# Cross-attention maxima added as three bfloat16 parts instead of two float32r parts

## The chip, the cores and the metric

The kernel is one launch on one core of a Trainium2 chip. The metric is the device time of that core in microseconds, as the median over several runs. Five engines share the work: TensorE (PE, with its weight loads shown apart as PEld), VectorE (DVE), ScalarE (ACT), GpSimd (POOL) and SyncE (SP), which here issues the DMAs. Each engine runs its own list of instructions, and the lists are tied together by semaphores.

## The reference

The kernel computes one decoder layer on 128 sequences of 128 tokens with 256 features. All three parts are added to the residual `x`:

```
x = x + self_attention(layernorm(x))               # 16 heads of 16, no mask
x = x + cross_attention(layernorm(x), ctx, ctx, mask)
x = x + ffn(layernorm(x))                          # 256 -> 1024 -> 256, ternary weights, GELU, layernorm inside

# cross-attention
scores = einsum('bhqd,bhkd->bhqk', Q, K) / sqrt(d_k)
scores = where(mask == 0, 1e-9, scores)            # mask: one row of keys, the same for all
attn   = softmax(scores)                           # exp(scores - max over keys) / sum
out    = einsum('bhqk,bhkd->bhqd', attn, V)
```

The softmax needs the maximum over the keys of every query and head. It is this maximum, negated, that the change handles.

## The kernel before

The sequences are taken in 32 groups of four (G = 4). Each group goes through self-attention, cross-attention and the FFN, and the three stages of different groups run side by side. All instructions are written out in a fixed order (`tc.manual_schedule()`): the string `ORDER` has one letter for each small step, `A` for a step of attention, `n`, `k`, `c` and `f` for the steps that prepare self-attention, prepare the keys of cross-attention, prepare its queries, and do the FFN of an earlier group. One pass over `ORDER` is one period: four rows of self-attention and four of cross-attention, a row being one sequence with all 16 heads. On each engine the instructions stand in the order in which this string emits them.

For a row, attention works in these steps, each emitted in one go:

- `maxima`: TensorE forms the scores with queries on the partitions (L562; in cross-attention after a mask term in bfloat16, L551), DVE takes the maximum over the keys, negated (L573), and writes it to `negm` (L579 for cross, L584 for self).
- `transposed_scores`: TensorE forms the scores again with the keys on the partitions (L620); in cross-attention DVE writes the constant into the masked places (`copy_predicated`, L630).
- `transposed_maxima`, for the row after: TensorE transposes `negm` into `pn`, a quarter of the one PSUM bank of `ps_av` (L589). For self-attention DVE adds it into the queries (`q_max`, L594). For cross-attention ACT copies it, rounded to float32r, to `first` (L604), and DVE forms `negm_t`: `pn` itself in the partitions of the first part, and `pn - first` in those of the second part (L606).
- `weights`: in cross-attention TensorE adds the maxima to the scores in PSUM with 16 small matmuls against the constant `add_max` (L644), four heads in each of four strips of 32 partitions. Then ACT takes the exponentials (L653, two halves).
- `outputs`: TensorE multiplies with the values into `av`, the same `ps_av` bank (L665), and ACT copies it out (L668).

`negm` has eight places of four heads in each strip; in cross-attention two of them hold the same maxima twice, so that the transposed tile holds the value twice, in different partitions. `add_max` picks and sums these partitions for each head.

The pools that matter are small. `ps_s` has room for the two score tiles of one row alone, so scores of the next row wait until the exponentials (or the maxima) have read the last ones. `ps_mm` has three banks, which all products of the projections and the FFN take in turn: `pq`, `pk`, `pv`, `po`, `pt`, `ph` (GELU on ACT, L392), `pg` (transposes L414, emptied by ACT L422 and DVE L424) and `py`. `ps_av` has one bank. The residual add of the output projection is DVE at L360, the statistics for the norms are DVE at L217 and L218, the copy of the values is L314 and that of the keys ACT at L300.

Of the kernel before, what the change touches and what calls it, by code (L numbers as in the profile page):

```python
# [18 lines left out]
F32 = mybir.dt.float32  # L19
F32R = mybir.dt.float32r  # L20
BF16 = mybir.dt.bfloat16
I32 = mybir.dt.int32
AF = mybir.ActivationFunctionType
ALU = mybir.AluOpType
AX = mybir.AxisListType
PSUM = bass.MemoryType.PSUM

P = 128
# [9 lines left out]
S4 = 4  # L38
# [21 lines left out]
def tile_decoder_layer(ctx: ExitStack, tc: tile.TileContext, a: dict, out: bass.AP):  # L60
    nc = tc.nc
    n_groups = a["x"].shape[0] // G

    const = ctx.enter_context(tc.tile_pool(name="const", bufs=1))
# [3 lines left out]
    p_att = ctx.enter_context(tc.tile_pool(name="p_att", bufs=2))  # L68
# [4 lines left out]
    ps_av = ctx.enter_context(tc.tile_pool(name="ps_av", bufs=1, space=PSUM))  # L73
# [32 lines left out]
    ident_strips = ident.rearrange("p (s r) -> p s r", s=S4)  # L106
# [4 lines left out]

    add_max = const.tile([P, 4, P], F32R, name="add_max")
    row_of = const.tile([P, 3], F32, name="row_of")
    for n in range(4):
        for i in range(2):
            rows = ident_strips[:, :, 4 * i + n]
            nc.vector.tensor_reduce(row_of[:, i : i + 1], rows, AX.X, ALU.add)
        nc.vector.tensor_tensor(row_of[:, 2:3], row_of[:, 0:1], row_of[:, 1:2], ALU.add)  # L120
        nc.vector.tensor_copy(add_max[:, n], row_of[:, 2:3].to_broadcast([P, P]))


    max_row = const.tile([P, CC, 2], F32, name="max_row")
# [1 line left out]
    for e in range(2):  # L126
        half = ident_strips[:, :, (1 - e) * HD : (1 - e) * HD + CC]
        nc.vector.tensor_reduce(max_rows[:, e : e + 1], half, AX.XY, ALU.add)
        for o in range(CC):
            nc.vector.tensor_reduce(max_row[:, o, e : e + 1], half[:, :, o], AX.X, ALU.add)  # L130
    minus_second = const.tile([P, 1], F32, name="minus_second")
    nc.vector.tensor_reduce(minus_second, ident_strips[:, :, 4:8], AX.XY, ALU.add, negate=True)

# [59 lines left out]
    rows = p_one.tile([P, S4, P], I32, name="rows", tag="g_0")  # L195
# [5 lines left out]
    least = const.tile([P, 1], F32, name="least")  # L201
# [337 lines left out]
    def score_tiles(name):  # L539
        return [ps_s.tile([P, 2, 4, P], F32, name=name, tag="s") for _ in range(2)]  # L540

    def maxima(stage, b, j):

        qt, kt = ready[stage, b]["q"], ready[stage, b]["k"]
        tok = slice(j * P, (j + 1) * P)
        s = score_tiles("s")
        if stage == "cross":
            for c in range(S4):
                for r in range(S4):
                    strip = slice(r * 32, (r + 1) * 32)  # L550
                    nc.tensor.matmul(  # L551
                        s[r // 2][c * 32 : (c + 1) * 32, r % 2],
                        ident_b[strip],
                        never[strip, c, None, :].to_broadcast([32, 4, P]),
                        start=True,
                        stop=False,
                        skip_group_check=True,
                    )
        for o in range(CC):
            for r in range(S4):  # L560
                strip = slice(r * 32, (r + 1) * 32)
                nc.tensor.matmul(  # L562
                    s[r // 2][:, r % 2, 2 * o : 2 * o + 2],
                    qt[strip, o, tok],
                    kt[strip, o, :, tok],
                    start=(stage == "self"),
                    stop=True,
                    skip_group_check=True,
                )

        mx = p_stat.tile([P, S4, 4, 2], F32, name="mx", tag="mx")[:, :, :, 0]
        for half in range(2):
            nc.vector.tensor_reduce(  # L573
                mx[:, 2 * half : 2 * half + 2], s[half], AX.X, ALU.max, negate=True
            )
        negm = negms[stage]
        if stage == "cross":
            twice = mx[:, :, None, :].to_broadcast([P, S4, 2, 4])
            nc.vector.tensor_scalar(negm[:, :, 0:2], twice, least, None, ALU.min)  # L579
        else:  # L580
            halves = negm.rearrange("p s a b -> p s (a b)").rearrange("p s (h d) -> p s h d", d=HD)
            heads = mx.rearrange("p s (o e) -> p s o e", e=2)
            for e in range(2):
                nc.vector.tensor_copy(halves[:, :, 1 - e, 0:CC], heads[:, :, :, e])  # L584
        return negm

    def transposed_maxima(stage, b, j, negm):
        pn = ps_av.tile([P, 4, P], F32, name="pn", tag="av")[:, 3]
        nc.tensor.transpose(pn, negm.rearrange("p s k n -> p (s k n)"), ident)  # L589
        if stage == "self":  # L590
            qt = ready[stage, b]["q"][:, :, j * P : (j + 1) * P]
            q_max = p_att.tile([P, CC, 2, P], F32, name="q_max", tag="q_max", bufs=1)
            for e in range(2):
                nc.vector.scalar_tensor_tensor(  # L594
                    q_max[:, :, e],
                    pn[:, None, :].to_broadcast([P, CC, P]),
                    max_rows[:, e : e + 1],
                    qt,
                    ALU.mult,
                    ALU.add,  # L600
                )
            return q_max
        first = p_att.tile([P, P], F32R, name="first", tag="q_max", bufs=1)
        nc.scalar.copy(first, pn)  # L604
        negm_t = p_att.tile([P, P], F32R, name="negm_t", tag="negm_t")
        nc.vector.scalar_tensor_tensor(  # L606
            negm_t, first.bitcast(F32), minus_second, pn, ALU.mult, ALU.add
        )
        return negm_t

    def transposed_scores(stage, b, j, added):
# [68 lines left out]
    def attention():  # L680
        w_t = added = None
        for i in range(-1, 2 * G * (n_groups + 1) + 1):
            here, following, before = row(i), row(i + 1), row(i - 1)
            cross = i % (2 * G) >= G
            if following:
                negm = maxima(*following)
            if i >= 0:
                yield
            if before:
                outputs(*before, w_t)  # L690
            if i >= 0:
                yield
            if here:
                s = transposed_scores(*here, added)
                if not cross:
                    w_t = weights(here[0], s, None)
            if i >= 0:
                yield
            added_here = added
            if following:  # L700
                added = transposed_maxima(*following, negm)
            if i >= 0:
                yield
            if cross and i >= 0:
                if here:
                    w_t = weights(here[0], s, added_here)
                yield
# [76 lines left out]
```

## Time and profile before

| | us |
|---|---|
| time, median of 3 runs | 2844.08 |
| lowest and highest of them | 2841.91, 2845.41 |
| the profiled execution: time | 2845.54 |
| the profiled execution: span | 2843.5 |
| mean granted TensorE clock in it | 0.98 of full |
| PE busy | 2723.7 (96%) |
| DVE busy | 2045.6 (72%) |
| ACT busy | 1546.9 (54%) |
| POOL busy | 1371.8 (48%) |

The profile comes from one execution of the program. A group is all instructions of one line, engine and operation; its row gives the busy time of all, the mean of one in ns, and the idle time of the engine just before them with what ended it. A timeline row gives the start in us from the span's start, the duration, the engine, the line, the tiles written and read, how many instructions were merged, and in brackets an idle time before them with its cause. The ends of matmuls are modelled, so a busy TensorE is not one at its peak; starts are the firmer numbers. The chain is the work that ended last, followed back from the end through what released each step.

### The profile page before, as it was taken

The page shows a single profiled execution, that of the slowest core. Times are in us where ns is not written, and L with a number is a line of the kernel's source. Part 1 is how long each engine was busy: PE and PEld are TensorE (multiplying, and loading weights), DVE is VectorE, ACT ScalarE, POOL GpSimd, SP SyncE. Part 2 cuts the span into 40 slices and gives each one's busy share as a digit, 9 for nine tenths or more (in the row PEclk, how much of TensorE's full clock was granted, in tenths as well). Part 3 has the DMA queues.
Part 4 walks back from the last instruction along what each step waited for, and adds up shares of the span by engine and source line. Part 5 has one row for each costly group of instructions (what it writes and reads, how often), then busy time and mean ns, then how long its engine had stood idle before and what let it go on. Part 6 is the DMA issues. An engine that isn't in the chain of part 4 may idle for free.

```text
span 2843.5 us, 76860 instructions
## 1 busy us (share of the span) xinstructions
PE 2723.7 (96%) x32797; PEld 1965.4 (69%) x32797; DVE 2045.6 (72%) x3788; ACT 1546.9 (54%) x2369; POOL 1371.8 (48%) x1425
## 2 busy tenths in 40 slices
PE   4789999999999999999999999999999999999985
PEld 2456777777777777777777777777777777777664
DVE  4457777787777778777777877777777777787663
ACT  0245555655655565555556556555655655566443
POOL 1225455554545555454545545454544545455343
PEclk8799999999999999999999999999999999999988
DMA  2112211211221121122112112211211221121111
GB/s 82 31 32 48 55 37 43 56 44 44 56 55 33 47 55 40 47 55 55 33 47 55 40 47 55 56 32 49 55 40 47 55 54 32 49 52 33 43 24 31
DMA packets 110948, 131.38 MB, mean 46 GB/s; under 512 B 32657, under 2 KB 69393, under 8 KB 110609
## 3 DMA queue, kind: packets, MB, share of 16 engines
q1 hardware_dynamic: 110608, 126.48, 18.2%
q8 instruction: 259, 4.24, 0.6%
q14 instruction: 81, 0.66, 0.1%
HBM read 71.91 MB, written 18.87 MB: 32 GB/s over the span
## 4 chain that ended last, share of the span: by engine, by line
PE 93%; DVE 3%; DMA 1%; POOL 1%; issue 1%; ACT 1%; SPq 0%; POOLq 0%; ACTq 0%; DVEq 0%
PE st L620 10%; PE s L562 10%; PE av L665 9%; PE py L437 9%; PE po L278 9%; PE ph L385 8%; PE pv L278 8%; PE pq L266 8%; PE pk L266 8%; PE pg L414 4%; PE pt L246 3%; PE st L644 3%; PE s L551 2%; PE pn L589 1%; DVE mx L573 1%
## 5 line engine op out<-in xcount | busy, mean ns | idle before, releaser
L573 DVE TENSOR_REDUCE mx<-s 128x8 f32<-128x1024 f32 x512 | 600.7, 1215 | 73.7 <-PE s L562 71.5
L653 ACT ACTIVATE w_t<-st 128x1024 f32<-128x1024 f32 x512 | 496.6, 1023 | 223.5 <-PE st L620 195.6
L223 POOL TENSOR_SCALAR rstd<-agg 128x4 f32<-128x4 f32 (+1 forms) x160 | 38.1, 238 | 1172.2 <-DVE agg L218 1170.3
L228 POOL TENSOR_SCALAR xn<-x,agg,rstd 128x256 f32<-128x256 f32 x384 | 464.2, 1221 | 10.0
L630 DVE COPY_PREDICATED_SCALAR st<-masked_t,masked_score 128x1024 f32 x256 | 315.7, 1279 | 64.5 <-PE st L620 61.0
L422 ACT ACTIVATE g<-pg,ln_w 128x256 fp32r<-128x256 f32 x512 | 211.4, 477 | 214.4 <-PE pg L414 211.0
L668 ACT COPY raw<-av 128x512 f32<-128x512 f32 x256 | 150.0, 586 | 302.9 <-PE av L665 302.6
L562 PE MATMUL s<-kt,qt 32*128 32x256 f32 x4096 | 301.2, 406 | 1.7 <-ACT w_t L653 1.7
L356 POOL TENSOR_TENSOR o_raw<-o_raw,factors 128x256 f32<-128x256 f32 x256 | 178.8, 726 | 252.5 <-DMA factors<-by_head 196.6
L665 PEld LDWEIGHTS av<-w_t,v 128*32 128x32 f32 x8192 | 211.6, 110 | 118.0 <-issue 26.0
L665 PE MATMUL av<-w_t,v 128*32 128x128 f32 x8192 | 281.2, 278 | 7.2 <-DVE negm_t L606 1.5
L228 POOL TENSOR_SCALAR g<-g,agg,rstd 128x1024 f32<-128x1024 f32 x64 | 276.8, 4324 | 6.7
L385 PE MATMUL ph<-w_fc,xn 128*128 128x512 f32 x1024 | 275.1, 411 | 1.2 <-ACT g L392 1.2
L437 PE MATMUL py<-w_proj,g 128*128 128x256 f32 x2048 | 272.2, 289 | 0.3 <-DVE g L424 0.2
L437 PEld LDWEIGHTS py<-w_proj,g 128*128 128x128 f32 x2048 | 254.9, 194 | 14.7 <-issue 9.6
L562 PEld LDWEIGHTS s<-kt,qt 32*128 32x128 f32 x4096 | 189.1, 187 | 108.1 <-issue 58.3
L424 DVE SCALAR_TENSOR_TENSOR g<-pg,ln_w,g 128x256 fp32r<-128x256 f32 x512 | 216.8, 476 | 32.0 <-ACT g L422 30.0
L385 PEld LDWEIGHTS ph<-w_fc,xn 128*128 128x128 f32 x1024 | 188.6, 192 | 55.2 <-DVE g L228 9.6
L314 DVE COPY v<-pv 128x512 f32<-128x512 f32 x128 | 86.3, 674 | 149.5 <-PE pv L278 149.5
L594 DVE SCALAR_TENSOR_TENSOR q_max<-pn,max_rows,qt 128x256 f32<-128x256 f32 x256 | 110.6, 474 | 111.8 <-PE pn L589 111.8
L392 ACT ACTIVATE g<-ph 128x512 f32<-128x512 f32 x256 | 146.2, 597 | 65.0 <-PE ph L385 64.2
L360 DVE TENSOR_TENSOR x<-x,po 128x512 f32<-128x512 f32 x128 | 87.5, 684 | 120.2 <-PE po L278 120.2
(113 smaller groups left out, 4748.6 us busy)
## 6 DMA issues: line engine op xcount, KB each, us to landing
o_raw<-raw SPq DMA_DIRECT2D x512, 64.0 KB
factors<-by_head SPq DMA_DIRECT2D x128, 256.0 KB
x<-in_x_dram SPq DMA_DIRECT2D x32, 512.0 KB
ctx_t<-in_ctx_t_dram SPq DMA_DIRECT2D x32, 512.0 KB
out_dram<-x SPq DMA_DIRECT2D x32, 512.0 KB
sums<-raw SPq DMA_DIRECT2D x128, 16.0 KB
by_head<-r SPq DMA_DIRECT2D x64, 32.0 KB
raw<-in_w_fc_t_dram SPq DMA_DIRECT2D x1, 1024.0 KB
```

What stands on the lines that cost most here:

```text
L228: engine.tensor_scalar(dst[:, j], src[:, j], agg[:, j, 0:1], rstd[:, j : j + 1], ALU.subtract, ALU.mult)
L266: nc.tensor.matmul(out, w[:, c, o * P : (o + 1) * P], src_t[:, c], start=(c == 0), stop=(c == CC - 1))
L278: nc.tensor.matmul(rows[:, j], src_t[:, c, (j0 + j) * P : (j0 + j + 1) * P], w[:, c], start=(c == 0), stop=(c == CC - 1),)
L385: nc.tensor.matmul(ph, xn_parts[i][:, c, (j0 + j) * P : (j0 + j + 1) * P], w_fc[:, c, n * 512 : (n + 1) * 512], start=((i, c) == terms[0]) ...
L424: nc.vector.scalar_tensor_tensor(parts[1][:, f0 + f], pieces[:, f], scales[f], parts[0][:, f0 + f].bitcast(F32), ALU.mult, ALU.subtract,)
L437: nc.tensor.matmul(rows[:, j], parts[i][:, f, j * P : (j + 1) * P], w_proj[:, f], start=((i, f) == terms[0]), stop=((i, f) == terms[-1]),)
L562: nc.tensor.matmul(s[r // 2][:, r % 2, 2 * o : 2 * o + 2], qt[strip, o, tok], kt[strip, o, :, tok], start=(stage == "self"), stop=True, sk ...
L573: nc.vector.tensor_reduce(mx[:, 2 * half : 2 * half + 2], s[half], AX.X, ALU.max, negate=True)
L620: nc.tensor.matmul(s[r // 2][:, r % 2, n], kt[strip, n // 2, n % 2, tok], added[strip, n // 2, n % 2] if stage == "self" else qt[strip, n ...
L630: nc.vector.copy_predicated(s[half].rearrange("p r n q -> p (r n) q"), masked_t[:, None, :].to_broadcast([P, 8, P]), masked_score[:, :, No ...
L653: nc.scalar.activation(w_t[:, 2 * half : 2 * half + 2], s[half], AF.Exp)
L665: nc.tensor.matmul(av[32 * r : 32 * r + 32, n], v[:, j, head : head + 32], w_t[:, r, n], start=True, stop=True)
```

## The change

The negated maximum of cross-attention is written to three places of `negm` instead of two, and split into three bfloat16 parts instead of two float32r ones. ACT copies `pn`, rounded to bfloat16, to `first`. DVE forms `rest`, which is `pn` less `first` in the partitions of the second and third part and `pn` itself in the others, and keeps it in PSUM, in another quarter of the bank of `pn`. ACT copies `rest`, rounded, to `second`, and DVE forms `negm_t` from `rest`, less `second` in the partitions of the third part. `add_max` and `negm_t` are bfloat16, so the matmuls of L644 are bfloat16. The set-up builds `add_max` from three rows for each head, and two columns of signs instead of one.

```
-    add_max = const.tile([P, 4, P], F32R, name="add_max")
-    row_of = const.tile([P, 3], F32, name="row_of")
+    add_max = const.tile([P, 4, P], BF16, name="add_max")
+    row_of = const.tile([P, 4], F32, name="row_of")
     for n in range(4):
-        for i in range(2):
-            rows = ident_strips[:, :, 4 * i + n]
-            nc.vector.tensor_reduce(row_of[:, i : i + 1], rows, AX.X, ALU.add)
-        nc.vector.tensor_tensor(row_of[:, 2:3], row_of[:, 0:1], row_of[:, 1:2], ALU.add)
-        nc.vector.tensor_copy(add_max[:, n], row_of[:, 2:3].to_broadcast([P, P]))
+        rows = ident_strips[:, :, n:12:4]
+        nc.vector.tensor_reduce(row_of[:, n : n + 1], rows, AX.XY, ALU.add)
+        nc.vector.tensor_copy(add_max[:, n], row_of[:, n : n + 1].to_broadcast([P, P]))
...
-    minus_second = const.tile([P, 1], F32, name="minus_second")
-    nc.vector.tensor_reduce(minus_second, ident_strips[:, :, 4:8], AX.XY, ALU.add, negate=True)
+
+    minus = const.tile([P, 2], F32, name="minus")
+    for i in range(2):
+        rows = ident_strips[:, :, 4 * (i + 1) : 12]
+        nc.vector.tensor_reduce(minus[:, i : i + 1], rows, AX.XY, ALU.add, negate=True)
...
-            twice = mx[:, :, None, :].to_broadcast([P, S4, 2, 4])
-            nc.vector.tensor_scalar(negm[:, :, 0:2], twice, least, None, ALU.min)
+            thrice = mx[:, :, None, :].to_broadcast([P, S4, 3, 4])
+            nc.vector.tensor_scalar(negm[:, :, 0:3], thrice, least, None, ALU.min)
...
-        pn = ps_av.tile([P, 4, P], F32, name="pn", tag="av")[:, 3]
+        av = ps_av.tile([P, 4, P], F32, name="pn", tag="av")
+        pn = av[:, 3]
...
-        first = p_att.tile([P, P], F32R, name="first", tag="q_max", bufs=1)
+        first = p_att.tile([P, P], BF16, name="first", tag="first", bufs=1)
         nc.scalar.copy(first, pn)
-        negm_t = p_att.tile([P, P], F32R, name="negm_t", tag="negm_t")
-        nc.vector.scalar_tensor_tensor(
-            negm_t, first.bitcast(F32), minus_second, pn, ALU.mult, ALU.add
-        )
+        rest = av[:, 2]
+        nc.vector.scalar_tensor_tensor(rest, first, minus[:, 0:1], pn, ALU.mult, ALU.add)
+        second = p_att.tile([P, P], BF16, name="second", tag="second", bufs=1)
+        nc.scalar.copy(second, rest)
+        negm_t = p_att.tile([P, P], BF16, name="negm_t", tag="negm_t")
+        nc.vector.scalar_tensor_tensor(negm_t, second, minus[:, 1:2], rest, ALU.mult, ALU.add)
         return negm_t
```

## Prediction

> **What bounds the kernel now.** I read the first page from the top: busy time, the chain, the groups.
>
> ```profile
> PE 2723.7 (96%) x32797; PEld 1965.4 (69%) x32797; DVE 2045.6 (72%) x3788; ACT 1546.9 (54%) x2369; POOL 1371.8 (48%) x1425
> ...
> PE 93%; DVE 3%; DMA 1%; POOL 1%; issue 1%; ACT 1%; SPq 0%; POOLq 0%; ACTq 0%; DVEq 0%
> ```
>
> TensorE is the bound, and the chain stays on it for 93% of the span. It works its instructions off in program order, so every stall put in front of it is lost, and every nanosecond taken from it is won only if nothing else is late by as much. The shares of DVE (72%) and ACT (54%) say that there is room on average. They do not say whether there is room at the place of the edit, so I next took the groups by form, for the instructions that the diff touches.
>
> ```profile
> L644 PE MATMUL st<-negm_t,add_max 32*128 32x128 f32 x2048 | 88.4, 284 | 8.6 <-DVE st L630 8.4
> L606 DVE SCALAR_TENSOR_TENSOR negm_t<-first,minus_second,pn 128x128 fp32r<-128x128 f32 x128 | 41.5, 324 | 40.1 <-ACT first L604 40.1
> L604 ACT CAST first<-pn 128x128 fp32r<-128x128 f32 x128 | 33.6, 263 | 116.0 <-PE pn L589 116.0
> ```
>
> 128 times a span (4 rows of cross-attention in each of 32 groups) ACT copies `first`, then DVE makes `negm_t`. The starts in the trace repeat every 83.17 us; at least 28 of the 32 repeats of each of the four places have the same lag from `first` to `negm_t`. So the timeline of one period, from 990 to 1028 us, stands for nearly all.
>
> **The change part by part: TensorE.** The 16 pairs of load and matmul at L644 go from float32r to bfloat16. In the timeline such a block starts at 1010.78 and the next matmul at 1011.38, 0.60 us. The only bfloat16 block (L551, 16 pairs) starts at 1014.27 and is followed at 1014.64, 0.37 us, but its loads have 32 columns and not 128. Upper bound of the gain: 0.60 - 0.37 = 0.23 us a block, 29 us over 128. Lower bound: the loads, not the products, set L644's beat. They take 0.53 us for 16, 33 ns each, and the float32 block at L620 has the same beat (0.98 us for 32). If bfloat16 loads no faster, nothing is won. A loss I exclude: 32-column loads take 88 ns in bfloat16 at L551 and 110 ns in float32 at L665. Taking that ratio, a fifth off, I say 0.1 us a block. The Trainium skill (TensorE: Matmul & The Clock Gate, "Weight-path perf modes") speaks for more: loads of 128 weights that are not FP32 may go by a fast path, about twice as fast measured. Half of 0.53 us would be 0.27 us, so the upper bound would hold. No row here shows a 128-column bfloat16 load, so I keep the row's value, and 0.23 for the range. It matters little, for the reason below.
>
> **DVE and ACT.** One DVE instruction and one ACT copy are added 128 times. Nearest rows: 324 ns (L606) and 263 ns (L604), with about 0.03 us at each hand-over (`first` ends at 1000.26, `negm_t` starts at 1000.29). As busy time that is 41 and 34 us on engines with room. A write into PSUM in place of SBUF has L630 as its row (1279 ns for 1024 elements, where L573, which only reads PSUM, takes 1215), so nothing is added for it. What counts is order. Before, DVE had one instruction, late, and ACT one, early, with nobody waiting on the way. Now DVE makes `rest`, ACT must wait for it with `second`, and DVE must wait for that with `negm_t`. Both engines take their instructions in program order, so all that is queued behind waits too. From the place of the old `negm_t`: rest 0.33, hand-over 0.03, second 0.27, hand-over 0.03: DVE's followers come 0.65 us later. ACT's followers come behind `second`, wherever DVE's backlog puts it. That nothing overtakes is stated by the Trainium skill (the same page, "Engine queue depths": ScalarE and VectorE are strict FIFO). The trace keeps program order too, but shows no instruction that could have overtaken and did not. If they could pass, the stalls below would be about zero and the sum would be the TensorE gain alone; I take the rule.
>
> **Place 0.**
>
> ```profile
> 992.91 0.32 DVE L606 SCALAR_TENSOR_TENSOR negm_t<-first,minus_second,pn 128x128 fp32r<-128x128 f32 x1
> 993.14 2.35 DVE L573 TENSOR_REDUCE mx<-s 128x8 f32<-128x1024 f32 x2
> ...
> 995.40 1.31 PE L620 MATMUL st<-qt,kt 32*128 32x128 f32 x32
> ```
>
> The maxima L573 follow at once, and L620 overwrites the scores that they read. L620 takes 1.31 us here against 1.17 elsewhere: it already waits 0.14 for the second maximum. DVE 0.65 later means TensorE 0.65 later.
>
> **Place 1.**
>
> ```profile
> 1000.00 0.26 ACT L604 CAST first<-pn 128x128 fp32r<-128x128 f32 x1
> 1000.22 1.94 ACT L653 ACTIVATE w_t<-st 128x1024 f32<-128x1024 f32 x2
> ...
> 1002.00 0.65 PE L551 MATMUL s<-never,ident_b 32*32 32x512 bf16 x16
> ```
>
> DVE is idle, but the exponentials L653 stand right behind `first`. They now wait for rest and second: from 1000.22 to about 1000.86. L551 takes the banks that they read and is already held (0.65 us against 0.43). TensorE: +0.63.
>
> **Place 2.**
>
> ```profile
> 1007.91 2.48 DVE L630 COPY_PREDICATED_SCALAR st<-masked_t,masked_score 128x1024 f32 x2 [1.01 <-PE st L620]
> 1010.29 0.34 DVE L606 SCALAR_TENSOR_TENSOR negm_t<-first,minus_second,pn 128x128 fp32r<-128x128 f32 x1
> ...
> 1008.17 0.27 ACT L604 CAST first<-pn 128x128 fp32r<-128x128 f32 x1 [0.39 <-PE pn L589]
> 1009.10 0.60 ACT L392 ACTIVATE g<-ph 128x512 f32<-128x512 f32 x1 [0.67 <-PE ph L385]
> 1010.02 0.60 ACT L392 ACTIVATE g<-ph 128x512 f32<-128x512 f32 x1 [0.32 <-PE ph L385]
> 1010.64 1.28 ACT L394 ACT_TABLE_LOAD   x1
> 1011.93 1.94 ACT L653 ACTIVATE w_t<-st 128x1024 f32<-128x1024 f32 x2
> ```
>
> This is the dearest. `rest` stands behind the two masking instructions until 1010.29, so `second` holds ACT until 1010.92. The two GELUs that ran inside that stretch come after it, and so 1010.85 to 1011.94; table load to 1013.24; exponentials to 1015.19 instead of 1013.87. L551 starts at 1014.27 and needs the second half at its third matmul: TensorE +0.93. The GELUs' own banks are asked for at 1012.15 and 1013.04, after 1011.45 and 1011.94, so nothing more is added.
>
> **Place 3.**
>
> ```profile
> 1024.42 0.29 DVE L606 SCALAR_TENSOR_TENSOR negm_t<-first,minus_second,pn 128x128 fp32r<-128x128 f32 x1
> 1024.63 0.68 DVE L360 TENSOR_TENSOR x<-x,po 128x512 f32<-128x512 f32 x1
> ...
> 1025.66 0.60 PE L414 MATMUL pg<-ident,g 128*128 128x128 f32 x4
> ```
>
> `first` is done at 1023.17, `rest` can start at 1024.42. L360 frees the bank of the second pg, at 1025.31 now and 1025.97 then; L414's loads follow, so it starts near 1026.08: +0.42. The exponentials end at 1026.89 instead of 1025.48, under the shifted L562 (1027.05 + 0.42), so they cost nothing more.
>
> **The sum.** 0.65 + 0.63 + 0.93 + 0.42 = 2.63 us a period. Of the TensorE gain only one block in four survives: those at 999.52, 1010.78 and 1022.79 bring TensorE earlier to a stall whose end is set by ACT or DVE, so theirs is lost; the one at 1037.55 keeps 0.1. Net 2.53 us. 29 regular periods make 73 us, three irregular ones at the ends, half as dear, 4: +77 us.
>
> **Edits costed at nothing.** The set-up drops reductions and sums of `row_of` on DVE, but DVE then idles 1.85 us for the DMA of the bias at 8.28 us, and TensorE waits behind that; were this cover gone, at most some 3 us would be won. L579 writes 48 columns instead of 32, 0.02 us, with 0.5 us and more before its transpose; uncovered 128 x 0.02 = 3 us. The buffer of `first` is no longer shared with `q_max`: at place 0 it started as soon as ACT was free, so no wait goes. `av` is held 0.65 us longer: freed at 993.9, asked for at 994.38; uncovered, up to 0.65 us a row. No DMA is added or moved, so SP's queue stays as it is, and so does POOL's.
>
> The profiled execution took 2845.5 us (span 2843.5), 1.5 above the median of 2844.08. The sum is an increment and stands on the median: 2844 + 77 = 2921.
>
> **The rivals.** (a) Faster, if the two extra hand-overs run in idle time and the bfloat16 blocks all count: 128 x 0.23 = 29 us, 2815. It decides if L573 at place 0 and the exponentials at places 1 to 3 have 0.65 us of slack or more; the two waits already seen (L620 at 1.31, L551 at 0.65) speak against it, the low ACT share for it. (b) Half the stalls: TensorE finds places 2 and 3 covered, for instance as `rest` and `second` are shorter than their rows. 1.3 us x 32 = 42: 2886. (c) Dearer: each hand-over nearer 0.9 us because of the new PSUM write, and the late exponentials and GELUs at place 3 also hold L562 and the next bank: 3.5 x 32 = 112: 2956. (d) The change does not do what it says, bfloat16 pairs being as slow as float32r: 2921 + 3 = 2924, inside the main case.
>
> **How the numbers follow.** A measurement of this kernel can tell about 0.2%, 5.7 us, from no change. Main case with (d) 0.72, its own range 2900 to 2940; (b) 0.12; (c) 0.10; (a) 0.06. Range 2882 to 2952: it reaches to (b), whose middle it takes in, and nearly to (c). Faster 0.05, same 0.02, slower 0.93.
>
> **What would show it.** TensorE's stretches lengthen at the four places: L620 at place 0 near 1.95 us, L551 at place 1 near 1.3 and at place 2 near 1.35; idle time before the loads L414 for L360. DVE idles about 0.3 us before each `negm_t` for `second`; ACT idles up to 2.2 us before `second` at place 2. The period grows from 83.17 to 85.7 us, and the chain's share on ACT and DVE grows. Wrong, if the L644 block is far under 0.37 us and the period does not grow, or if the GELUs run ahead of `second`.

## The result, and the profile after

The changed kernel takes 2921.82 us (median of 5 runs, 2919.06 to 2926.82) against 2844.08 before: 78 us slower, a ratio of 1.0283 with a 95% interval of 1.0268 to 1.0298. Of the five executions of the kernel before that the ratio could draw on, one took 3413.41 us, in a slower state of the chip, and is left out. The prediction was 2921, with a range of 2882 to 2952. The mean granted clock of TensorE is 0.977 in the profiled execution, against 0.980 before, and full from 215 to 2620 us in both, so the clock does not make the difference.

The page after, busy time and the chain (line numbers are up to four higher than before: the scores L620 are L624, the block L644 is L648, the exponentials L653 are L657):

```profile
PE 2731.4 (94%) x32797; PEld 1941.0 (66%) x32797; DVE 2105.8 (72%) x3909; ACT 1562.9 (54%) x2497; POOL 1355.2 (46%) x1425
...
PE 69%; DVE 17%; ACT 10%; DMA 1%; issue 1%; POOL 1%; SPq 0%; POOLq 0%; DVEq 0%; ACTq 0%
```

The shares of busy time hardly move; DVE and ACT still look as if they had room. The chain shows the difference: TensorE falls from 93% of it to 69%, and DVE and ACT, 4% together before, now have 27%. The groups of the touched instructions:

```profile
L648 PE MATMUL st<-negm_t,add_max 32*128 32x128 bf16 x2048 | 53.8, 218 | 9.6 <-DVE st L634 9.5
L612 DVE SCALAR_TENSOR_TENSOR negm_t<-second,minus,pn 128x128 bf16<-128x128 bf16 x128 | 44.5, 348 | 42.6 <-ACT second L610 42.6
L608 DVE SCALAR_TENSOR_TENSOR pn<-first,minus,pn 128x128 f32<-128x128 bf16 x128 | 42.5, 332 | 41.2 <-ACT first L606 41.2
L610 ACT CAST second<-pn 128x128 bf16<-128x128 f32 x128 | 33.9, 265 | 185.8 <-DVE pn L608 185.8
```

`rest` (which the profile names pn, the tile that it lies in) takes 332 ns, against 324 for the old `negm_t`, which was written to SBUF, so the write into PSUM costs nothing to speak of. ACT sits idle for 185.8 us before `second`, waiting for DVE, and DVE another 42.6 us, 0.33 each time, before `negm_t`. That is the idle time of two engines that queue other work behind it. The timeline at place 2, ACT and then TensorE:

```profile
1034.78 0.27 ACT L610 CAST second<-pn 128x128 bf16<-128x128 f32 x1 [2.23 <-DVE pn L608]
1034.94 1.09 ACT L393 ACTIVATE g<-ph 128x512 f32<-128x512 f32 x2
1036.05 1.28 ACT L395 ACT_TABLE_LOAD   x1
1037.34 1.94 ACT L657 ACTIVATE w_t<-st 128x1024 f32<-128x1024 f32 x2
...
1038.42 0.39 PE L552 MATMUL s<-never,ident_b 32*32 32x512 bf16 x2 [0.23 <-ACT w_t L657]
1039.33 0.43 PE L552 MATMUL s<-never,ident_b 32*32 32x512 bf16 x14 [0.52 <-ACT w_t L657]
```

The two GELUs, which before ran apart as their inputs came, now run back to back behind `second`, then the table load, then the exponentials. The mask block of the next row starts at 1038.42, stops after two matmuls and goes on at 1039.33, when the exponentials have read the second half. At places 0, 1 and 3:

```profile
1016.35 0.35 DVE L612 SCALAR_TENSOR_TENSOR negm_t<-second,minus,pn 128x128 bf16<-128x128 bf16 x1 [0.33 <-ACT second L610]
1016.62 2.35 DVE L574 TENSOR_REDUCE mx<-s 128x8 f32<-128x1024 f32 x2
...
1018.18 0.49 PE L624 MATMUL st<-qt,kt 32*128 32x128 f32 x4
1019.02 0.73 PE L624 MATMUL st<-qt,kt 32*128 32x128 f32 x16 [0.35 <-DVE mx L574]
...
1024.16 0.27 ACT L610 CAST second<-pn 128x128 bf16<-128x128 f32 x1 [0.42 <-DVE pn L608]
1024.32 1.95 ACT L657 ACTIVATE w_t<-st 128x1024 f32<-128x1024 f32 x2
...
1026.32 0.43 PE L552 MATMUL s<-never,ident_b 32*32 32x512 bf16 x14 [0.53 <-ACT w_t L657]
...
1051.08 0.66 PE L415 MATMUL pg<-ident,g 128*128 128x128 f32 x4 [0.50 <-DVE x L361]
```

Each names the same releaser as the prediction did: the maxima, the exponentials, the residual add.

TensorE has the same matmuls in the same order in all the kernels told of here, so the starts of one period can be laid over each other (places 0 to 3 are its four rows of cross-attention), from the `pn` of place 0 (990.83 before, 1013.61 after) to that of the next period. The table gives, in us, by how much TensorE falls behind the kernel before (minus: gets ahead) in each stretch, the gain of the block that lies in it included. The stretches end at the keys' product after place 0 (996.64 before), at L562 after place 1 (1002.58), at `av` after place 2 (1017.78), at L562 after place 3 (1027.05) and at the next period; the last holds the fourth block.

| kernel | place 0 | place 1 | place 2 | place 3 | rest | sum |
|---|---|---|---|---|---|---|
| predicted for the change | +0.65 | +0.63 | +0.93 | +0.42 | -0.10 | +2.53 |
| the change | +0.69 | +0.63 | +0.92 | +0.45 | -0.20 | +2.49 |
| bfloat16 blocks alone | 0.00 | -0.06 | -0.25 | -0.23 | -0.21 | -0.75 |
| hand-overs alone, float32r | +0.69 | +0.63 | +0.93 | +0.45 | 0.00 | +2.71 |
| `second` on DVE | +0.72 | -0.06 | -0.25 | +0.75 | -0.19 | +0.96 |
| both steps moved | +0.69 | -0.06 | +0.37 | +4.94 | -0.20 | +5.73 |
| moved, DVE's step further | +0.69 | -0.06 | -0.15 | -0.23 | +0.36 | +0.62 |
| long chain at place 2 alone | 0.00 | -0.06 | +0.96 | -0.23 | -0.21 | +0.46 |
| one part | -0.14 | -0.06 | -0.26 | -0.26 | -0.21 | -0.93 |
| one part, place 1 on DVE | -0.14 | -0.21 | -0.26 | -0.26 | -0.20 | -1.08 |

2.49 us a period over 32 periods are 80 us; the measured difference is 78 by the medians and 80 by the ratio.

### The profile page after: what moved, and what is told of

Read it like the earlier page. It is cut to its first block, busy times and chain, and to the rows that moved or that the text cites. A ratio compares the mean times of both kernels' runs of the same rounds, so it can differ in the third digit from the quotient of the medians.

```text
span 2920.8 us, 76981 instructions
## 1 busy us (share of the span) xinstructions
PE 2731.4 (94%) x32797; PEld 1941.0 (66%) x32797; DVE 2105.8 (72%) x3909; ACT 1562.9 (54%) x2497; POOL 1355.2 (46%) x1425
## 4 chain that ended last, share of the span: by engine, by line
PE 69%; DVE 17%; ACT 10%; DMA 1%; issue 1%; POOL 1%; SPq 0%; POOLq 0%; DVEq 0%; ACTq 0%
PE st L624 10%; PE py L438 9%; PE s L563 9%; PE av L669 8%; PE po L279 6%; DVE st L634 6%; PE pk L267 5%; PE pq L267 5%; PE ph L386 5%; ACT w_t L657 4%; PE pv L279 4%; PE pg L415 4%; DVE mx L574 3%; DVE stats L218 3%; PE pt L247 2%; ACT kt L301 1%
## 5 line engine op out<-in xcount | busy, mean ns | idle before, releaser
L657 ACT ACTIVATE w_t<-st 128x1024 f32<-128x1024 f32 x512 | 496.8, 1025 | 202.4 <-PE st L624 195.9
L229 POOL TENSOR_SCALAR g<-g,agg,rstd 128x1024 f32<-128x1024 f32 x64 | 260.8, 4075 | 6.7
L624 PE MATMUL st<-qt,kt 32*128 32x128 f32 x4096 | 168.2, 287 | 16.3 <-DVE mx L574 16.2
L624 PEld LDWEIGHTS st<-qt,kt 32*128 32x128 f32 x4096 | 137.2, 188 | 57.4 <-DVE mx L574 34.0
```

The lines of the kernel that those rows point to most:

```text
L229: engine.tensor_scalar(dst[:, j], src[:, j], agg[:, j, 0:1], rstd[:, j : j + 1], ALU.subtract, ALU.mult)
L624: nc.tensor.matmul(s[r // 2][:, r % 2, n], kt[strip, n // 2, n % 2, tok], added[strip, n // 2, n % 2] if stage == "self" else qt[strip, n ...
L657: nc.scalar.activation(w_t[:, 2 * half : 2 * half + 2], s[half], AF.Exp)
```

## The experiments

The theory: the loss is the order on ACT and DVE, that is, what is queued behind the two waits, place by place; the time of TensorE's blocks counts only where nothing else ends the stall. The rivals: the parts add up independently; or the added work itself costs (busy time, traffic in PSUM, bfloat16).

**The bfloat16 blocks alone.**

Against the kernel before:

```
-    add_max = const.tile([P, 4, P], F32R, name="add_max")
+    add_max = const.tile([P, 4, P], BF16, name="add_max")
...
-        first = p_att.tile([P, P], F32R, name="first", tag="q_max", bufs=1)
+        first = p_att.tile([P, P], BF16, name="first", tag="first", bufs=1)
...
-        negm_t = p_att.tile([P, P], F32R, name="negm_t", tag="negm_t")
+        negm_t = p_att.tile([P, P], BF16, name="negm_t", tag="negm_t")
```

> The kernel before with its two parts, but first, negm_t and add_max in bfloat16: the TensorE half of the change alone, no added hand-over. (The maximum is then added to 16 bits; the same for all keys of a query, so it divides out of the softmax.) Theory, that stalls are set by the order on ACT and DVE: a block of 16 takes 0.34 us instead of 0.60, 0.26 less; at place 1 it is lost (the exponentials stand behind first on ACT), at places 2 and 3 it counts, and of the fourth block 0.2 counts. 0.7 us a period, 32 periods: 23 us faster, about 2821. Rival, that every nanosecond of TensorE counts: 128 x 0.26 = 33 us faster, 2811. Rival, that bfloat16 costs elsewhere: 2844.

Measured: 2820.13 us, ratio 0.992 (0.9906 to 0.9935), 22 us faster than before on the same chip (2842.43). The row of the table shows which blocks count: those at places 2 and 3 and the fourth. At place 1 the block itself is 0.26 shorter, and 0.20 of that is given back at L551, as the exponentials stand behind `first`. Had all four counted in full, the time would be 33 us lower, 2809, and the lowest run was 2816.79.

**The hand-overs alone.**

Against the changed kernel:

```
-    add_max = const.tile([P, 4, P], BF16, name="add_max")
+    add_max = const.tile([P, 4, P], F32R, name="add_max")
...
+        parts = p_att.tile([P, 2, P], F32R, name="parts", tag="q_max", bufs=1)
+        first, second = parts[:, 0], parts[:, 1]
...
-        negm_t = p_att.tile([P, P], BF16, name="negm_t", tag="negm_t")
+        negm_t = p_att.tile([P, P], F32R, name="negm_t", tag="negm_t")
```

> The changed kernel with all three parts, rest in PSUM and both hand-overs, but first, second, negm_t and add_max in float32r: the other half of the change alone (first and second share the buffer of q_max, for space). Theory: the ends of the stalls are set by ACT and DVE, so the slower blocks at places 1, 2 and 3 vanish in them; stalls 0.69 + 0.63 + 0.95 + 0.45 = 2.7 us a period, 87 us over before, about 2931. Rival, that the parts add up independently: 78 us of the change plus 33 us of the lost TensorE gain, 2955. Rival, that the stalls come from bfloat16: near 2844.

Measured: 2930.28 us, ratio 1.0311 (1.0296 to 1.0327). The four places are those of the change to within 0.01 us, although the blocks are slower. So bfloat16 gains 22 us when it comes alone and 8 us (2930.28 less 2921.82, measured at different times) when the hand-overs are there: three blocks of four only lengthen the wait in front of a stall.

**`second` on DVE.**

Against the changed kernel:

```
-        nc.scalar.copy(second, rest)
+        nc.vector.tensor_copy(second, rest)
```

> The changed kernel with second copied by DVE instead of ACT: same data, one hand-over to ACT and back taken away, DVE has one instruction more. Theory: ACT is not held any more, so the stalls at places 1 and 2 go (and place 2 keeps its 0.26); DVE's followers still come about 0.57 us later, so places 0 and 3 stay (+0.57 and +0.35), the fourth block keeps 0.2: about +0.46 us a period, 15 us over before, 2859. Rival, that the added DVE work or the write of rest into PSUM is what costs: 2922 or more.

Measured: 2873.0 us, ratio 1.0111 (1.0096 to 1.0126). The places of ACT behave as expected: 1 and 2 are back at the values of the bfloat16 blocks alone. So 49 us of the change go with ACT's wait, though DVE has more to do. The 14 us over the expectation lie on DVE, here at place 3:

```profile
1034.87 0.30 DVE L608 SCALAR_TENSOR_TENSOR pn<-first,minus,pn 128x128 f32<-128x128 bf16 x1
1035.20 0.29 DVE L610 CAST second<-pn 128x128 bf16<-128x128 f32 x1
1035.53 0.35 DVE L612 SCALAR_TENSOR_TENSOR negm_t<-second,minus,pn 128x128 bf16<-128x128 bf16 x1
1035.79 0.68 DVE L361 TENSOR_TENSOR x<-x,po 128x512 f32<-128x512 f32 x1
```

The residual add starts 0.92 us after the first of the three, where it started 0.21 after the old `negm_t`: 0.71 later and not 0.57. Each of the three reads what the last one wrote and starts 0.03 to 0.04 us after its end, while the residual add, which does not need `negm_t`, starts 0.09 us before the end of the third. Place 0 loses 0.72. Place 3 loses 0.75 where the expectation had 0.35: DVE also arrives there 0.2 later, measured from `pn` (its copy of the values starts 0.02 us before `pn`'s matmul, and 0.21 before it in the kernel before). The traces fit that this is what is left of the 0.7 us of place 2: between the two places DVE idled 0.36 us before the maxima and 0.11 before the masking in the kernel before, and at neither here, so that slack is used up. No run varies it alone.

**The same instructions, moved.**

Against the changed kernel, for places 1 to 3; the two instructions are emitted by `last_parts`, after the exponentials:

```
+        def last_parts():
+            nc.scalar.copy(second, rest)
+            nc.vector.scalar_tensor_tensor(negm_t, second, minus[:, 1:2], rest, ALU.mult, ALU.add)
...
+            later.append(last_parts)
...
                     w_t = weights(here[0], s, added_here)
+                    for last_parts in later:
+                        last_parts()
```

> The changed kernel with the same instructions in another order: at places 1 to 3, second and the last step of negm_t are emitted after the exponentials of the row in hand instead of before them; place 0 is as in the change. Theory: places 1 and 2 cost nothing any more (place 2 keeps its 0.26), place 3 about 0.1 for rest alone, place 0 its 0.69, the fourth block keeps 0.2: +0.33 us a period, 11 us over before, 2855. Rival, that the added instructions cost wherever they stand (busy time, PSUM traffic, hand-overs): about 2922.

Measured: 3025.4 us, ratio 1.0639 (1.0622 to 1.0657): 170 us over the expectation, and on the side of neither. DVE's timeline at place 2, with ACT's beside it, shows where it begins; TensorE's two waits for the maxima that follow are below them:

```profile
1069.94 0.35 DVE L614 SCALAR_TENSOR_TENSOR negm_t<-second,minus,pn 128x128 bf16<-128x128 bf16 x1 [3.54 <-ACT second L613]
...
1067.81 1.94 ACT L664 ACTIVATE w_t<-st 128x1024 f32<-128x1024 f32 x2
1069.64 0.27 ACT L613 CAST second<-pn 128x128 bf16<-128x128 f32 x1
...
1076.30 0.49 PE L631 MATMUL st<-qt,kt 32*128 32x128 f32 x4 [1.31 <-DVE mx L574]
1077.43 1.86 PE L631 MATMUL st<-qt,kt 32*128 32x128 f32 x28 [0.64 <-DVE mx L574]
```

I had moved the ACT half out of the way and not looked at what the move does to DVE: its last step now stands behind a copy that itself stands behind the exponentials, and DVE waits 3.54 us with the statistics and the next maxima queued behind. In all, DVE's idle time before `negm_t` grows from 42.6 to 217.1 us. Places 0 and 1 came out as expected (+0.69 and -0.06); what follows place 2, up to the end of place 3, came to +5.31 in the two columns. The instructions are those of the change, one for one, and in this order the kernel takes another 104 us.

Not all of that is waiting. Right behind the two waits of TensorE the granted clock (the number after the busy times) is halved for 3.4 us:

```profile
1077.70:1081.10 3.40, 3.40 (x33) 2.82 (x30) 3.37 (x5) 0.00 (x0) 3.40 (x5) 0.50 0.00 0
```

Between 215 and 2620 us this kernel has 27 such stretches, 102 us in all, one in each period; no other kernel here has any there. If TensorE does half the work in them, they cost about 50 us (an estimate), near half of the 104. The theory had no such term. That the waits bring the lower clock about is likely from where it stands, but no run shows it.

**Moved, with DVE's step moved on as well.** Against the run just above, at places 2 and 3 the last step goes to right before the next maxima (`before_maxima` is emptied in `maxima`, ahead of the two reductions):

```
+        elif j == 1:
+            later += [copy_second, last_part]
+        else:
+            later.append(copy_second)
+            before_maxima.append(last_part)
```

> A third order of the changed kernel's instructions: at places 2 and 3 second stands behind the exponentials on ACT, and the last step of negm_t on DVE stands right before the next maxima instead of right behind second's emission (which made DVE wait for the exponentials in the order tried before); place 1 as in that order; place 0 as in the change. Theory: place 0 +0.69, place 1 about +0.07, place 2 -0.26, place 3 about +0.2 (rest before the residual add, and av waits 0.3 for negm_t), the fourth block -0.2: +0.5 us a period, 16 us over before, about 2858. Rival, that moving second behind the exponentials is itself the loss: near 3025 again.

Measured: 2864.06 us, ratio 1.0081 (1.0065 to 1.0096). Places 1 to 3 are free now. The +0.36 of the last stretch is a new wait at `av`, for the bank that holds `rest` until `negm_t` has read it. It puts `av` 0.55 us later, where the expectation had 0.3; the gain of the fourth block goes off it:

```profile
1030.43 0.34 DVE L620 SCALAR_TENSOR_TENSOR negm_t<-second,minus,pn 128x128 bf16<-128x128 bf16 x1
1030.82 1.08 PE L686 MATMUL av<-w_t,v 128*32 128x128 f32 x32 [0.48 <-DVE negm_t L620]
```

Three orders of the same instructions give 3025, 2922 and 2864 us. So the added work itself is not what costs: it is the same in all three.

**The long chain at place 2 alone.**

Against the changed kernel:

```
+        if j != 2:
+            negm_t = p_att.tile([P, P], BF16, name="negm_t", tag="negm_t")
+            nc.vector.scalar_tensor_tensor(negm_t, first, minus[:, 0:1], pn, ALU.mult, ALU.add)
+            return negm_t
```

> The changed kernel with the long chain (rest, second, negm_t) only for the third row of cross-attention, place 2; the other rows go from first to negm_t in one DVE step. (Their third partitions then add pn - first once more, the same for all keys of a query.) Theory, that each place has its own stall and they add up: place 2 as in the change (-0.26 + 0.30 + 0.91 = +0.95 us), the other places as with the bfloat16 blocks alone (0 to -0.06, -0.26, -0.2): +0.45 us a period, 14 us over before, about 2857. Rival, that the stalls are one backlog that any of them pays (or that late ACT is absorbed by the next): 2900 or more, or under 2835.

Measured: 2857.8 us, ratio 1.0057 (1.0042 to 1.0072). Place 2 has the +0.9 of the change, and the other places those of the bfloat16 blocks alone. So the stall at place 2 stands by itself, and with the runs above, which take away places 1 and 2 or 1 to 3 and keep place 0, the stalls of the change add up.

**One part.** The first experiment pointed further. The constant that is added to the scores of a query and head is the same for all its keys, and the sum by which the output is divided is made of the same exponentials. So its rounding divides out, and one bfloat16 part is enough as long as the exponentials stay in range.

Against the changed kernel (`negm` also holds the maxima once only, and `add_max` is built from one row for each head):

```
-        first = p_att.tile([P, P], BF16, name="first", tag="first", bufs=1)
-        nc.scalar.copy(first, pn)
-        rest = av[:, 2]
...
-        nc.vector.scalar_tensor_tensor(negm_t, second, minus[:, 1:2], rest, ALU.mult, ALU.add)
+        nc.scalar.copy(negm_t, pn)
```

> One part alone: ACT copies pn, rounded to bfloat16, to negm_t, and no DVE instruction is left in the step. (The maximum is added to 8 bits; the same for all keys of a query, so it divides out of the softmax.) Theory: the gain of the bfloat16 blocks (0.76 us a period as measured with two parts), and at place 0 the maxima come 0.33 us earlier on DVE, which takes away the 0.14 that L620 already waited there before: 0.90 us a period, 29 us under before, about 2814. Rival, that a DVE instruction less is worth nothing: as with two parts, 2820.

Measured: 2812.88 us, ratio 0.9898 (0.9882 to 0.9915). Place 0 gains 0.14, which is just the wait that L620 had there before; the other places stay as with two parts.

**One part, the copy at place 1 on DVE.**

Against the kernel with one part:

```
-        nc.scalar.copy(negm_t, pn)
+        if j == 1:
+            nc.vector.tensor_copy(negm_t, pn)
+        else:
+            nc.scalar.copy(negm_t, pn)
```

> The kernel with one part, with the copy of pn at place 1 made by DVE, which is idle there, instead of by ACT. Theory: what is left of a stall at place 1 (the bfloat16 block wins 0.26 there and 0.20 is given back) is set by the exponentials behind that copy on ACT; without it they start when the copy of the keys is done, about 0.2 us earlier: 0.2 us a period, 6 us under the 2813 of one part, about 2807. Rival, that something else ends the wait of L551 there (the banks, POOL, the keys): 2813.

Measured: 2807.27 us, ratio 0.9883 (0.9863 to 0.9903). At place 1 TensorE now keeps 0.21 of its 0.26, 0.15 more than with the copy on ACT; 32 times that is 5 us, and the medians differ by 5.6. The intervals of the two ratios overlap, so that this last step gains rests on the table more than on the medians. It is the fastest of all, 115 us under the change.

## Why the prediction was right

- **The bound.** That TensorE's stalls are lost time held: behind place 3 nothing is won back (the last stretch is 0.00 for the hand-overs alone, and for the change only the fourth block's own gain). That one period stands for the whole run held too: the sums of the table, times 32, are within 2.2 us of the measured difference in every row (+31 us by the table and 31 measured with `second` on DVE, -35 and -36 for the fastest).
- **Places 0 to 3.** All four stalls came at the instruction, behind the releaser and within 0.04 us of the size that was worked out. The sum within 1 us of the forecast is partly luck: the four stalls came 0.06 us larger in all, the surviving block gained 0.10 more, and the two nearly cancel. The two kernels that do half of the change each bear them out: the hand-overs alone have the four stalls and no gain, the bfloat16 blocks alone have no stall.
- **"Of the TensorE gain only one block in four survives".** Right in the mechanism, wrong in the size of the term. A block of 16 takes 0.335 us from its first load to the next group's, 0.26 less than before. I had said 0.1, and the upper bound of 0.23 was too low as well. The step that failed is the choice of the row: L551's loads have 32 columns, and I took from them that bfloat16 loads are a fifth faster. The loads before and after show this:

```profile
L644 PEld LDWEIGHTS st<-negm_t,add_max 32*128 32x128 f32 x2048 | 69.3, 186 | 57.7 <-DVE st L630 51.2 <-issue 6.5
L648 PEld LDWEIGHTS <-add_max 32*128 32x128 bf16 x2048 | 30.9, 93 | 58.5 <-issue 58.1
```

93 ns against 186 for the same 32 x 128 in float32r: twice as fast, as the Trainium skill states for loads of 128 weights that are not FP32 (TensorE: Matmul & The Clock Gate, "Weight-path perf modes"). The measurement sides with the rule there and against my row; float32r does not get the fast load, its 186 ns being those of float32 (187 ns at L562). Loads and products changed type together, so how the two share the 0.26 us is not shown. It cost the forecast little, since the surviving block was 0.20 instead of 0.10: 3 us of 2921.
- **The cover.** That `av` would not wait for the bank held 0.65 us longer was right for the change; once the last step was moved further, it did wait, 0.55 us a period.
- **Strict order on ACT and DVE.** Only the rule stood for it before. The change shows it on ACT: the products of both GELUs at place 2 are done by 1034.09, yet the GELUs start at 1034.94, behind `second` and its wait of 2.23 us. The three orders show it on DVE: work behind a waiting instruction waits too, 3.54 us at the worst.
- **Rivals.** (a) fell at the four places, where no slack of 0.65 us was to be had; (b) fell at places 2 and 3, which were not covered (+0.92 and +0.45); (c) fell with `rest` at 332 ns; (d) fell with the block at 0.335 us.

## What to carry to other kernels

Cost a split across two engines by what is queued behind each wait, at each place where it stands, and not by the busy time it adds: here 0.6 us of work for each row, on engines idle for 28% and 46% of the time, made the kernel 78 us longer in one order and 22 us in another. A saving on the engine that is the bound counts only where nothing else ends the next stall, so look for that stall first. Before making a step exact, ask whether its error divides out: a softmax's maximum needs to be the same for all keys, not precise.

## What was not expected of the hardware

The weight loads of 32 x 128 float32r and bfloat16 differ by the factor of two above, and a block of 16 takes 0.335 us instead of 0.60. A chain of three dependent DVE instructions of 0.3 us pushes the next one back by 0.71 us, as much as the detour by ACT (0.65 to 0.69): the hand-over between the engines itself, about 0.03 us, is not what costs here. And in the kernel with both steps moved the granted clock was halved for 3.4 us once in each period, right behind two waits of TensorE of 1.31 and 0.64 us.
